# Twelve groups of TensorE products whose results nobody reads, taken out of the last block of a four-layer kernel

## The chip, the cores and the metric

The kernel runs on one core of one Trainium2 chip, as one launch. The metric is the device time of that core in microseconds; several executions are measured and their median is given. One further execution is taken with the hardware profiler, and all profile lines come from that one.

## The reference, cut to what matters

The input `x` has 128 sequences of 64 tokens with 256 features. Four conditioned layers follow each other, each added to its own input:

```python
x = x + L0(x, cond_512, ...)      # self-attention, 16 heads, per-sequence modulated weights
x = x + L1(x, cond_512, ...)      # a bottleneck of 64 with per-sequence weights
x = x + L2(x, ids, states, ...)   # layer norms with gathered tables, then an MLP and a layer norm
x = x + L3(x, cond_512, ...)      # a rank-30 per-sequence weight
```

The change lies at the seam between the last two. The end of L2 and all of L3 are

```python
def _mlp_ln(s, W1, b1, W2, b2, g, b):
    h = jax.nn.silu(s @ W1 + b1) @ W2 + b2
    return _ln(h, g, b)                    # (h - mean) * rsqrt(var + eps) * g + b

U = (mu @ W_dec + b_dec).reshape(B, IN_DIM + 1, K)     # K = 30
param = jnp.einsum('bik,kj->bij', U, V)
out = jnp.einsum('bsd,bde->bse', x, param[:, :-1, :]) + param[:, -1, :][:, None, :]
```

## The kernel before, in words

The 8192 tokens are cut into 16 blocks of 512 tokens (8 sequences). A prologue computes all that depends on the condition alone. Then each block goes through `attention(blk)` (L0) and `rest(blk, ...)` (L1, L2, L3). Inside a block, a "tile" is 128 tokens, so there are four tiles, `tl` = 0 to 3; feature-major arrays are held in two halves, `c` = 0 and 1.

**Order of the work.** Nothing is issued while the Python functions run. Each call of `pe`, `dve`, `act`, `pool` or `load` records an operation in a `Plan`, with its estimated time, what it reads and writes, and the buffers it needs. `Plan.order()` then simulates the engines and picks, for each engine among the operations that could start now, the one with the lowest number `prio`: the block's number times 400, plus an entry of a table `TURNS` (one table for the prologue, the first, the second, the middle, the last but one and the last block). The resulting list is emitted as it is, so each engine executes its instructions strictly in that list's order. PSUM banks (four buffers called `bank`) go to operations in the order in which they are planned.

**The end of a block.** For the last block, where `quick` is true, the end of L2 and L3 run so:

- L1387 (PE): for each tile, the product of `s2` with `w2` into a bank; L1392 (DVE) adds `b2` and stores `x3[tl]`; L469 and L470 (DVE) compute its mean and variance into `mvy`.
- L474 and L476 (POOL) make `ry`, the reciprocal standard deviation of all four tiles; L1253 and L1254 (POOL) make `nry`, minus the mean times `ry`.
- L1259 (ACT), four times: `yn[tl]`, the normalized tile.
- L1403 and L1406 (POOL), per tile: the product with the gamma `lg`, and the sum with `x2[tl]`, which gives the residual stream token-major in `x3[tl]`.
- L1418 (PE): eight transposes of 128x128, first the four tiles of `c` = 0 and then the four of `c` = 1; L1424 (DVE), once for each `c`, scales by gamma and adds the residual, giving `x3T`.
- L1445 (PE): the products with `uT`, 32 small matmuls; L1456 (DVE) adds the bias into `zT`; L1471 (PE): the products with `vw` into four banks.
- L1479 (DVE), per tile: bank plus `x3[tl]`; L1483 (SP): the output DMA of that tile.

In the profile these buffers carry the name of the slot that they sit in: `uu`, `uv` and `p` are pools of slots that are inherited by `x3`, `h`, `s2` and others once their first use is over. So `uu` or `p` in a line is often `yn` or `x3`.

**The products that nobody reads.** The helper `keep(n, gate)` (L437 to L449) takes a bank, multiplies four columns of a value `gate` with the identity (L444), and then multiplies the identity with itself `n` times (L446). Nothing reads the bank afterwards. The L444 matmul waits until the gate's value is there. `keep` records its operation as one of the prologue, with the table entry -500, so it comes ahead of any operation of the last block that could start at the same moment on PE. In the last block it is called six times: with `n` = 4 for `mvy`, `ry` and `nry`, and with `n` = 3 for `yn[0]`, `yn[1]` and `yn[2]`. In fp32 each of these matmuls appears twice in the profile (2 and 8 for `n` = 4; 2 and 6 for `n` = 3).

Of the kernel before, what the change touches and what calls it, by code (L numbers as in the profile page):

```python
# [22 lines left out]
NTILE = T // 128  # L23
# [35 lines left out]
class Plan:  # L59
# [19 lines left out]
    def op(self, eng, took, emit, reads=(), writes=(), busy=None, claims=(), full=0.0, mode=0, pair=False, dma=0.0, table=0):  # L79


        k = self.noted[self.blk] = self.noted.get(self.blk, -1) + 1
        o = dict(eng=eng, took=took, busy=took if busy is None else busy, emit=emit, full=full, mode=mode, pair=pair, dma=dma, table=table)
        o.update(blk=self.blk, k=k, n=len(self.ops), deps=set(), turn=set(), bufs=[], new=[])
        for wr, us in ((False, reads), (True, writes), (False, [(b, "claim") for b in claims])):
            for u in us:
                buf, part = u if isinstance(u, tuple) else (u, None)
                if buf.fixed and part == "claim":
                    continue
                if not buf.seen:  # L90
                    o["new"].append(buf)
                elif buf.seen[0][0] is not o:
                    o["turn"].add(buf.seen[0][0]["n"])
                for other, p, w in buf.seen:
                    if other is not o and (w or wr) and (p is None or part is None or p == part):
                        o["deps"].add(other["n"])
                if wr or not buf.fixed:
                    buf.seen.append((o, part, wr))
                    if buf not in o["bufs"]:
                        o["bufs"].append(buf)  # L100
                        buf.left += 1
        self.ops.append(o)
# [117 lines left out]
    -30847 -21098 5029 39705 -29888 -33414 17870 15965 21160 18587 23602 29288 20398 29675 -32783 -14063 -2864 31417  # L220
    17450 17488 -15993 28657 -41896 -7536 -19666 21238 -40657 411 24862 11649 -23801 10654 8695 15478 -14178 -28768
    -42626 -13379 -20998 18401 -17670 15952 -3416 12222 20491 37701 1362 -22594 -9529 15406 6194 21828 27928 25779
    -10633 41137 464 10909 -44878 -11608 -42604 -45090 10155 -44468 -500 -500 -500 -500 -500 -500
    """,
    "first": """
    16883 -4343 14529 16216 12997 362 17988 20162 -39793 -680 16016 -20705 24354 5226 -12605 14786 19988 -2731 30982
# [85 lines left out]
def resid_chain(ctx: ExitStack, tc: tile.TileContext, a: dict, out: bass.AP, nblk: int = NBLK):  # L312
# [8 lines left out]
    nc = tc.nc  # L321
# [7 lines left out]
    ident = const.tile([128, 128], F32, name="ident", tag="ident")  # L329
# [100 lines left out]
    plan = Plan(kinds, turns, {"p1": list(HEIRS_1), "p2": list(HEIRS_2), "uu": list(HEIRS_U), "uv": list(HEIRS_V)})  # L430
    op = plan.op

    def pe(us, f, reads, writes, claims=(), full=1.0, mode=0):

        op("PE", us + 0.16, f, reads, writes, busy=us, claims=claims, full=full, mode=mode)

    def keep(n, gate):  # L437


        ps, blk = Buf("bank"), plan.blk  # L440
        plan.blk = -1

        def products():
            nc.tensor.matmul(ps.t[:, :4], ident, gate[1](), start=True, stop=True)  # L444
            for k in range(n):
                nc.tensor.matmul(ps.t[:, bass.ts(k, 128)], ident, ident, start=True, stop=True)  # L446

        pe(0.12 * n, products, [gate[0]], [ps])
        plan.blk = blk  # L449

    def dve(n, f, reads, writes, more=0.0, pair=False):

# [7 lines left out]
    def pool(us, f, reads, writes):  # L460
        op("POOL", us + 0.1, f, reads, writes, busy=us)
# [729 lines left out]
    def rest(blk, x1T, pw, oh, wdn, wup, tab, uT):  # L1191

        b0 = blk * NB
        quick = blk == nblk - 1
# [56 lines left out]
        def offset(mv, r, nr):  # L1251

            pool(0.24, lambda: nc.gpsimd.tensor_scalar(nr.t, mv.t[:, :, 0], -1.0, None, ALU.mult), [mv], [nr])  # L1253
            pool(0.24, lambda: nc.gpsimd.tensor_tensor(nr.t, nr.t, r.t, ALU.mult), [nr, r], [nr])  # L1254

        def normalize(dst, src, r, nr, tl):
            act(
                256,
                lambda: nc.scalar.activation(  # L1259
                    dst.t, src.t, AF.Identity, bias=nr.t[:, tl : tl + 1], scale=r.t[:, tl : tl + 1]  # L1260
                ),
                [src, r, nr],
                [dst],
                more=0.186,
            )

        x2, xn, h = ([Buf(k) for _ in range(NTILE)] for k in ("x2", "xn", "h"))
        for tl in range(NTILE):
            ps = Buf("bank")
# [32 lines left out]
        for dst, src in ((xnT, xn), (hnT, h)):  # L1302
            for c in range(C):
                ps = Buf("bank")
# [7 lines left out]
        for j, src, dst in ((1, xnT, gs), (2, xnT, xnT), (0, hnT, hnT)):  # L1312
            for c in range(C):
                ps = Buf("bank")
# [20 lines left out]
        for fc in range(C):  # L1335
            ps, th = Buf("bank"), Buf("tmp")
# [42 lines left out]
        mvy, ry, nry = Buf("mvy"), Buf("ry"), Buf("nry")  # L1379
        x3 = [Buf("x3") for _ in range(NTILE)]  # L1380
        yn = [Buf("h") for _ in range(NTILE)] if quick else x3
        for tl in range(NTILE):
            ps = Buf("bank")
# [9 lines left out]
            stats(x3[tl], mvy, tl)  # L1393
        rstd(mvy, ry)
        offset(mvy, ry, nry)
        if quick:
            for value in (mvy, ry, nry):
                keep(4, (value, lambda value=value: value.t.rearrange("p n k -> p (n k)")[:, :4] if value is mvy else value.t))
        for tl in range(NTILE):
            normalize(yn[tl], x3[tl], ry, nry, tl)  # L1400
            if quick and tl < NTILE - 1:
                keep(3, (yn[tl], lambda tl=tl: yn[tl].t[:, :4]))
            pool(0.65, lambda tl=tl: nc.gpsimd.tensor_tensor(x3[tl].t, yn[tl].t, lg, ALU.mult), [yn[tl]], [x3[tl]])  # L1403
            pool(
                0.65,
                lambda tl=tl: nc.gpsimd.tensor_tensor(x3[tl].t, x3[tl].t, x2[tl].t, ALU.add),  # L1406
                [x3[tl], x2[tl]],
                [x3[tl]],
            )
# [3 lines left out]
        for c in range(C):  # L1413
            ps = Buf("bank")
# [23 lines left out]
        ps, zT = Buf("bank"), Buf("zT")  # L1438
# [26 lines left out]
        for two in range(2):  # L1465
# [8 lines left out]
            for i in range(2):  # L1474
                tl = 2 * two + i
                n = blk * NTILE + tl
# [11 lines left out]
    for blk in range(nblk):  # L1488
        plan.blk = blk
        rest(blk, *attention(blk))  # L1490
# [118 lines left out]
```

## Time and profile before

| what | value |
|---|---|
| median of 3 runs | 900.8 us (897.63 to 904.46) |
| profiled execution, its own time | 894.98 us |
| span of that execution in the profile | 893.2 us |
| mean granted TensorE clock | 0.984 |
| PE busy | 830.2 us (93%) |
| DVE, POOL, ACT busy | 638.4, 608.0 and 446.9 us |
| last products of L1387 end | about 875.1 us after the span's start |
| first transposes of L1418 start | 884.52 us |
| last output DMA issued | 890.27 us |

The span runs from the first to the last instruction of the core; the profiled execution's own time is 1.78 us longer. Times in the views count from the span's start. "Granted clock" is the share of full speed that TensorE's throttle granted in a stretch. PE means matmuls, PEld the loads of their weights. A line number is that of the kernel before; in the changed kernel the lines after the helper are 14 lower, and those after the removed calls 19 lower. In the kernel before, the program's last PE instructions stand in this order: L1387, then six times L444 with its L446, then L1418, L1445 and L1471.

### The profile page before, as it was taken

How to read it: one execution, taken by the hardware profiler on the slowest of the kernel's cores; microseconds unless marked ns; L12 is line 12 of the kernel's file. 1: busy time of each engine (PE TensorE's matmuls, PEld its weight loads, DVE VectorE, ACT ScalarE, POOL GpSimd, SP SyncE). 2: the span in 40 equal slices, each digit the busy share in tenths (PEclk: the TensorE clock that was granted, in tenths of full speed). 3: DMA queues.
4: the chain of work that ended last, by engine and by line, in shares of the span. 5: the costliest groups of instructions: out<-in, count | busy, mean ns of one | idle time of the engine just before them, and what ended most of it. 6: DMA issues, size and time to landing. Idle time of an engine off the chain costs nothing.

```text
span 893.2 us, 24076 instructions
## 1 busy us (share of the span) xinstructions
PE 830.2 (93%) x9806; PEld 539.8 (60%) x9806; DVE 638.4 (71%) x1365; ACT 446.9 (50%) x825; POOL 608.0 (68%) x826
## 2 busy tenths in 40 slices
PE   4669999999999999999999999999999999999886
PEld 3548746656665756666566657566666667565435
DVE  3779867868685878777785858777776858586533
ACT  1454444545564555545555645555555556453330
POOL 5563673949687695959596886959595968845333
PEclk9889999999999999999999999999999999999998
DMA  8768742233423242332334232423324332102000
GB/s 252 210 160 251 243 127 64 67 85 103 123 84 116 73 119 82 95 94 73 117 88 125 85 111 69 128 77 92 101 74 117 84 97 84 48 11 64 1 24 25
DMA packets 62575, 90.24 MB, mean 101 GB/s; under 512 B 6328, under 2 KB 46200, under 8 KB 62464
## 3 DMA queue, kind: packets, MB, share of 16 engines
q1 hardware_dynamic: 57344, 71.92, 28.1%
q0 software_dynamic: 5120, 16.78, 6.0%
q8 instruction: 77, 1.26, 0.6%
q14 instruction: 34, 0.28, 0.1%
HBM read 75.44 MB, written 13.24 MB: 99 GB/s over the span
## 4 chain that ended last, share of the span: by engine, by line
PE 54%; POOL 18%; DVE 13%; ACT 6%; issue 5%; DMA 3%; SPq 0%; DVEq 0%; ACTq 0%; POOLq 0%
PE bank L1344 19%; PE sc L1071 4%; PE bank L982 4%; PE bank L1387 4%; PE bank L1015 4%; PE bank L1146 4%; DVE mt L1080 3%; POOL wdn L956 2%; PE sc L1121 2%; POOL kxe L1029 2%; PE bank L1058 2%; PE bank L1176 2%; POOL uu L1290 2%; PE bank L1317 1%; POOL xsT L925 1%
## 5 line engine op out<-in xcount | busy, mean ns | idle before, releaser
L1135 ACT ACTIVATE e<-sc 128x1024 f32<-128x1024 f32 x128 | 125.9, 1023 | 78.3 <-PE sc L1121 78.3
L1080 DVE TENSOR_REDUCE mt<-sc 128x8 f32<-128x1024 f32 x128 | 151.9, 1205 | 16.2 <-PE sc L1071 13.6
L1165 POOL TENSOR_TENSOR att<-ao,rz 128x256 f32<-128x256 f32 x45 | 28.1, 625 | 76.2 <-DVE rz L1162 75.9
L1326 DVE TENSOR_TENSOR uu<-uu,bank 128x512 f32<-128x512 f32 x96 | 63.9, 681 | 16.4 <-PE bank L1317 15.8
L1015 PE MATMUL bank<-wk,xsT 128*128 128x256 f32 x256 | 71.0, 413 | 0.9 <-POOL xsT L925 0.8
L1344 PE MATMUL bank<-uu,w_s 128*128 128x512 f32 x128 | 66.7, 604 | 0.8 <-DVE uu L1326 0.8
L1344 PE MATMUL bank<-uu,w_t 128*128 128x512 f32 x128 | 65.0, 618 | 0.5 <-DVE uu L1326 0.5
L1344 PE MATMUL bank<-x2T,w_x 128*128 128x512 f32 x128 | 64.7, 607 | 0.0
L1387 PE MATMUL bank<-w,uu 128*128 128x256 f32 x256 | 61.8, 385 | 1.9 <-DVE uu L1362 1.9
L1015 PEld LDWEIGHTS bank<-wk,xsT 128*128 128x128 f32 x256 | 48.8, 202 | 19.1 <-issue 11.1
L982 PE MATMUL bank<-osT,wo 128*128 128x512 f32 x128 | 59.2, 604 | 0.5 <-DVE osT L1181 0.5
L1344 PE MATMUL bank<-uu,w_h 128*128 128x512 f32 x128 | 58.7, 595 | 0.5 <-DVE uu L1326 0.4
L474 POOL TENSOR_SCALAR ry<-mvy 128x4 f32<-128x4 f32 (+1 forms) x19 | 4.4, 232 | 77.7 <-DVE mvy L470 77.6
L1090 ACT COPY mt<-mt 128x16 f32<-128x16 f32 x64 | 13.1, 204 | 84.4 <-DVE mt L1080 84.4
L469 DVE BATCH_NORM_STATS2 st<-uu 128x6 f32<-128x256 f32 x119 | 48.5, 418 | 8.1 <-ACT uu L1276 5.0
L1029 POOL TENSOR_TENSOR kxe<-kxe,kbr 128x256 f32<-128x256 f32 x64 | 46.8, 732 | 9.0 <-DVE kxe L1023 6.6
L1387 PEld LDWEIGHTS bank<-w,uu 128*128 128x128 f32 x256 | 45.9, 190 | 9.4 <-DVE uu L1362 3.1
L1023 DVE TENSOR_TENSOR kxe<-bank,dmk 128x256 f32<-128x256 f32 x64 | 26.8, 419 | 30.3 <-PE bank L1015 25.6
L956 POOL TENSOR_TENSOR wdn<-gdb,late 128x512 f32<-128x512 f32 x32 | 40.6, 1272 | 11.4 <-PE bank L1205 6.0
L940 POOL DMA_INDIRECT pw<-in_pw,idx x39 | 40.0, 1024 | 8.0 <-issue 7.4
L970 POOL TENSOR_TENSOR wup<-wup,ubb 128x512 f32<-128x512 f32 x32 | 40.6, 1269 | 3.7 <-DMA ubb<-ugub 1.5
L1103 ACT ACTIVATE mX<-bank,early 128x128 bf16<-128x128 f32 x64 | 23.6, 369 | 38.3 <-PE bank L1096 38.3
(217 smaller groups left out, 2135.9 us busy)
## 6 DMA issues: line engine op xcount, KB each, us to landing
xT<-in_xT SPq DMA_DIRECT2D x32, 256.0 KB
gdb<-dgdb SPq DMA_DIRECT2D x16, 512.0 KB
ubb<-ugub SPq DMA_DIRECT2D x32, 256.0 KB
wup<-ugub SPq DMA_DIRECT2D x32, 256.0 KB
dmk<-demod_k SPq DMA_DIRECT2D x30, 256.0 KB
out_x<-uu SPq DMA_DIRECT2D x35, 128.0 KB
ud<-uu SPq DMA_DIRECT2D x8, 512.0 KB
uT<-ud SPq DMA_DIRECT2D x16, 256.0 KB
```

Of the source, the lines that this page charges most:

```text
L469: dve(256, lambda: nc.vector.bn_stats(st.t, x.t), [x], [st])
L940: lambda tl=tl, n=n: nc.gpsimd.indirect_dma_start(out=pw[tl].t, out_offset=None, in_=a["pw"], in_offset=bass.IndirectOffsetOnAxis(ap=idx[: ...
L956: lambda w=w, dp=dp: nc.gpsimd.tensor_tensor(w(), gdb.t[:, :, 0:64], dp, ALU.mult),
L970: pool(1.25, lambda w=w: nc.gpsimd.tensor_tensor(w(wup), w(wup), w(ubb), ALU.add), [wup, ubb], [wup])
L982: nc.tensor.matmul(ps.t, owT[:, c, bass.ts(oc, 128)], osT.t[:, c, :], start=(c == 0), stop=(c == C - 1))
L1015: nc.tensor.matmul(ps.t[:, :F], xsT.t[:, c, bass.ts(tl, 128)], kwT[:, c, :], start=(c == 0), stop=(c == C - 1))
L1029: lambda: nc.gpsimd.tensor_tensor(kxe.t[:, :, 0:D], kxe.t[:, :, 0:D], heads(kinds["kbr"][0]), ALU.add),
L1080: lambda two=two: nc.vector.tensor_reduce(mt.t[:, two, 0:4], sc.t[:, two, :].rearrange("p q (g n) -> p q g n", g=4), AX.X, ALU.max),
L1135: lambda k=k: nc.scalar.activation(es[k].t, sc.t[:, 2 * k : 2 * k + 2, :], AF.Exp, scale=0.25),
L1326: lambda ps=ps, src=src, dst=dst, c=c: nc.vector.tensor_tensor(dst.t[:, c, :], src.t[:, c, :], ps.t, ALU.mult),
L1344: lambda ps=ps, w=w, src=src, fc=fc, c=c, n=n: nc.tensor.matmul(ps.t, w.t[:, c, bass.ts(fc, 128)], src.t[:, c, :], start=(n == 0 and c == ...
L1387: nc.tensor.matmul(ps.t[:, :F], s2.t[:, c, bass.ts(tl, 128)], w2.t[:, c, :], start=(c == 0), stop=(c == C - 1))
```

## The change

The helper `keep`, its six calls and its six table entries are taken out. The change is described as "the last block without the unread products; the orders of the last two blocks searched anew", but nothing else in the source differs: the tables of the last two blocks hold the same numbers in both kernels. When both kernels are built and their instructions are laid side by side, engine by engine, DVE, ACT, POOL and SP have the same instructions in the same order over the whole program; PE has the same order without the twelve rows of L444 and L446.

```diff
-    -10633 41137 464 10909 -44878 -11608 -42604 -45090 10155 -44468 -500 -500 -500 -500 -500 -500
+    -10633 41137 464 10909 -44878 -11608 -42604 -45090 10155 -44468
...
-    def keep(n, gate):
-
-
-        ps, blk = Buf("bank"), plan.blk
-        plan.blk = -1
-
-        def products():
-            nc.tensor.matmul(ps.t[:, :4], ident, gate[1](), start=True, stop=True)
-            for k in range(n):
-                nc.tensor.matmul(ps.t[:, bass.ts(k, 128)], ident, ident, start=True, stop=True)
-
-        pe(0.12 * n, products, [gate[0]], [ps])
-        plan.blk = blk
-
...
         rstd(mvy, ry)
         offset(mvy, ry, nry)
-        if quick:
-            for value in (mvy, ry, nry):
-                keep(4, (value, lambda value=value: value.t.rearrange("p n k -> p (n k)")[:, :4] if value is mvy else value.t))
         for tl in range(NTILE):
             normalize(yn[tl], x3[tl], ry, nry, tl)
-            if quick and tl < NTILE - 1:
-                keep(3, (yn[tl], lambda tl=tl: yn[tl].t[:, :4]))
```

In the built program the first four transposes now carry waits of their own: each waits for ACT's normalize of its tile. Before, only the fourth did, since the products ahead of it had waited for the other three.

## The prediction

> **What bounds the kernel now.** I read the page first: PE is busy 93% of the span, so TensorE bounds the kernel as a whole. But the change touches only the last 20 us, where PE's work is partly products without a reader, so the share of busy time says nothing here. I therefore took the chain that ended last, in order of time, for the tail; each row is a start, a length and what the chain passed through.
>
> ```profile
> 875.09 0.42 DVE p L1392
> ...
> 876.82 1.01 POOL ry L476
> 877.84 0.04 issue
> 877.88 0.39 PE bank L444 x2
> 878.26 1.54 PE bank L446 x8
> 879.81 0.22 PE bank L444 x2
> 880.03 1.91 PE bank L446 x8
> 881.94 0.18 PE bank L444 x2
> ...
> 884.68 0.45 PE bank L1418 x4
> 885.13 0.03 issue
> 885.16 1.42 DVE uu L1424 x2
> 886.58 0.04 issue
> 886.62 0.59 PE bank L1445 x24
> ```
>
> The reader is to see that from 877.88 to 884.4 the chain runs through nothing but the products of L444 and L446: they are not beside the path, they are the path. The transposes of L1418 stand behind them on an engine that works in order. What the transposes really need is shown by the timeline of ACT and POOL:
>
> ```profile
> 879.63 0.58 ACT L1259 ACTIVATE uu<-p,nry,ry 128x256 f32<-128x256 f32 x1
> ...
> 883.72 0.72 POOL L1406 TENSOR_TENSOR uu<-uu,p 128x256 f32<-128x256 f32 x1
> ```
>
> The four normalizes end at 878.74, 879.23, 879.72 and 880.21 (starts 878.14, 878.65, 879.14, 879.63; lengths 0.60 and 0.58). So the last input of the transposes exists at 880.21, and the first one runs at 884.52. In the view of waits over this stretch the same delay stands on the other side:
>
> ```profile
> DVE uu L1424 <- PE bank L1418: 9.0, 1, 9.0
> ```
>
> The products' own price depends on TensorE's clock, so the last view is PE in stretches of 3.41 us: the stretch, its length, PE's busy time with the number of instructions, the granted clock, and the share and rate of the DMAs:
>
> ```profile
> 868.32:871.73 3.41, 2.00 (x7) 1.00 0.00 0
> 871.73:875.15 3.42, 3.42 (x19) 1.00 0.00 0
> 875.15:878.56 3.41, 1.71 (x15) 1.00 0.00 0
> 878.56:881.97 3.41, 3.41 (x19) 0.50 0.02 5
> 881.97:885.39 3.42, 3.42 (x31) 1.00 0.00 0
> 885.39:888.80 3.41, 1.74 (x42) 1.00 0.00 0
> ```
>
> The clock changes at 878.56, 881.97 and 888.8, that is, in steps of one such stretch: a stretch that was busy for half its length (1.71) is followed by one at half speed, a stretch that was full by one at full speed. The products after the half-speed stretch run at full speed, and so do L1418, L1445 and L1471.
>
> [...]the stretch from 851.25 to 854.67 was busy for 2.13 us, half of it (1.06) transposes of L1308, and the next one ran at 0.50; the one from 868.32 with 2.00 us of plain products was followed by 1.00. [...]
>
> **The change part by part.** The order of the other four engines is the same in both built programs, and that of PE is the same without the twelve rows, so up to 874.8 the two kernels do the same work in the same order. I price everything before at nothing: the tables of the last two blocks are not altered, though the change's description speaks of searched orders.
>
> *Removed:* 12 rows in L444, 42 in L446, from 874.80 to 884.4. The first group (gate `mvy`, 1.4 us) lies in a gap in which PE has nothing else, and is worth nothing. The rest holds the transposes back.
>
> *What is late next:* the chain L1259. The fourth normalize lands at 880.21. The transposes of `c` = 0 for tiles 0 to 2 run before that, one by one as the normalizes come (0.5 us apart, which covers one cold transpose at 0.22 each). So one transpose of `c` = 0 and four of `c` = 1 are left at 880.25.
>
> *Added:* nothing is issued, but the tail loses its warm clock. PE has no work from 875.06 to 878.8, 3.7 us; then five of eight transposes are left. By the stretches above I take clock 0.50 for all that follows. What it costs, from rows at both clocks:
>
> - Transposes. Four L1058 transposes took 1.12 us at 0.50 (at 58.70) and 0.66 warm (at 783.17): 0.22 or 0.11 apart, and 0.46 or 0.33 for the last one's length. Cold, one transpose from its weight load to DVE's start is 0.23 + 0.46 + 0.04 = 0.73, so L1424 for `c` = 0 starts at 880.98 and ends at 881.69. The four of `c` = 1 end 4 x 0.22 = 0.88 later, at 881.83; L1424 for `c` = 1 runs from 881.87 to 882.58.
> - L1445. No cold row of it exists. Warm its last 24 take 0.59: 0.37 of issue and 0.22 of the last one's length. Bounds: 0.59 if only latency counts, 1.18 at plain doubling. I take 0.37 x 2 + 0.28 = 1.02, since the drain is not all clocked work (0.33 to 0.46, not to 0.66, above). Start 882.62, end 883.64.
> - L1456: 0.02 + 0.30 + 0.04, as before, to 884.00.
> - L1471. Again no cold row with all eight; warm 0.78 = 0.30 issue + 0.48. Bounds 0.78 and 1.56. I take 0.60 + 0.59 = 1.19, to 885.19; L1479 starts at 885.22.
>
> Before, L1479 starts at 888.40. The gain is 888.40 - 885.22 = 3.2 us; with both bounds at plain doubling 2.6 us (885.75), with L1445 and L1471 warm 4.0 us (884.38).
>
> *Cover for the rest.* L1479 also reads `x3[tl]`, whose last sum on POOL ends at 884.44, for tile 3; POOL's order does not depend on PE here. Tile 3 is reached about 1.1 us after L1479's first start (889.48 against 888.40), at 886.3, so 1.9 us of slack remain. In the warmest case, 884.38 + 1.1 = 885.5, it is still 1.0. From L1479 on (four adds, four output DMAs of 128 KB, no other transfer in flight) nothing changes: last DMA issued 890.27, span's end 893.2. No wait is added behind which anything queues: the three new waits on the first transposes hold only transposes back.
>
> Sum: span 893.2 - 3.2 = 890.0 us, own time 894.98 - 3.2 = 891.8 us. The median of the three runs before is 5.8 us above the profiled execution, so in medians I carry the difference over: 900.8 - 3.2 = 897.6 us. About 1% (9 us) is what a measurement of this kernel can tell from no change, and the runs before lie 6.8 us apart; the gain is a third of one per cent.
>
> **The rivals.**
>
> *The products were cheap in most executions.* [...]Warm, the groups cost 1.1, 1.1 and three times 0.90 (882.62 to 883.52) from 877.88: the transposes would start at 882.8 and not 884.5, so before would be 1.6 us faster than profiled, and the gain only 3.2 - 1.6 = 1.6 us: 899.2 us. [...]against: the profiled execution is cold.
>
> *The tail stays warm.* If the transposes[...] bring the clock to 1.00 by 882, the gain is 4.0 us, 896.8 us. Against: at most 1.76 us of cold transposes fall into that window, and the trace went cold after 1.71 and 2.13.
>
> *Slower: the clock falls lower than half.* PE's work from 880.25 on is, warm, about 0.66 for five transposes, 0.59 and 0.78, together 2.03 us; DVE's steps and the gaps are 1.15. Before has 888.40 - 880.25 = 8.15 us for it. The change loses from a slowing of (8.15 - 1.15) / 2.03 = 3.4 on, a granted clock under 0.29. [...]No stretch of this trace shows a clock under 0.50.
>
> *The change reaches further than the tail*, by the searched orders it speaks of. The side-by-side order excludes it[...].
>
> **How the numbers follow.** Cold tail against cold products 0.58 (897.6); products mostly warm before 0.27 (899.2); warm tail 0.08 (896.8); [...]something unseen 0.04. [...]the likeliest's own bounds are 896.8 to 898.2. A median of few runs that lie 6.8 us apart is uncertain by some 2 to 3 us, which I add below: 894.2 to 901.4. Faster by over 1% needs 9 us, three times the gain: 0.04, from the unseen and from the spread. Slower by over 1%: 0.02. Within 1%: 0.94.
>
> **What would show it right or wrong.** Right: no L444 or L446; the four L1259 end near 880.2; three transposes run singly between 878.8 and 880.2; the clock is 0.50 from about 878.6 on to the end; L1424 starts near 881.0, L1479 near 885.2, POOL's last sum still at 884.4, the span ends near 890.0. The step on the clock is wrong if L1471 takes 0.78 at 1.00; the step on POOL is wrong if L1479's last add is released by POOL; the whole is wrong if L1424 does not start before 884, or if spans differ before 874.8 by as much as the gain.

## The result and the profile after

| | before | after | ratio |
|---|---|---|---|
| first set, 14 runs each | 903.02 us | 901.59 us (897.82 to 904.63) | 0.9978 [0.9957, 0.9998] |
| second set (49 runs of before, 22 of after) | 893.09 us | 890.84 us (888.46 to 894.55) | 0.9976 [0.9964, 0.9987] |
| profiled execution, first set | 894.98 us, span 893.2 us | 902.43 us, span 900.6 us | |

The brackets hold 95% intervals. One of the 49 runs, 1070.64 us long at a granted clock of 0.753, is left out of the ratio. What was taken out are six groups with 54 rows in the profile, 12 of L444 and 42 of L446: the "twelve" of the title counts the rows of L444.

The change gains 0.2%, about 2 us. Its profiled execution was nevertheless 7.4 us longer than that of before. So spans must not be compared here; the tail must be. I count from the end of the last product of L1387 (L1373 after), which ends at 875.06 us in the profile of before and at 885.15 us in that of after: 10.1 us were lost ahead of any changed instruction. Times of the tail, and ends of spans counted from there, are taken from the unrounded records; the rows shown here can differ by 0.01 us.

The two rows of before between which the change lies:

```profile
871.34 3.73 PE bank L1387 x16
...
888.40 0.47 DVE p L1479 x2
```

The chain that ended last, after, in order of time (start, length, what it passed through):

```profile
881.43 3.73 PE bank L1373 x16
...
888.24 0.61 ACT uu L1245
...
890.37 1.34 PE bank L1399 x5
...
891.73 0.76 DVE uu L1405
...
892.54 0.91 PE bank L1426 x24
...
893.82 1.30 PE bank L1452 x8
...
895.16 0.47 DVE p L1460 x2
```

The products are gone from it: PE comes right behind the normalizes of ACT. L1460 starts at 895.16, 10.01 us after the last product of L1373; before it was 888.40 - 875.06 = 13.34. The forecast was 13.34 - 3.18 = 10.16. The view of waits has the same on its other side, 4.6 us instead of 9.0:

```profile
DVE uu L1405 <- PE bank L1399: 4.6, 1, 4.6
```

The clock, in stretches of 3.41 us, the length of the one at 0.50 in the profile of before (stretch, length, PE busy and instructions, granted clock, DMA share and rate):

```profile
884.36:887.77 3.41, 0.79 (x4) 1.00 0.00 0
887.77:891.18 3.41, 2.24 (x7) 0.50 0.00 0
891.18:894.59 3.41, 2.59 (x43) 0.50 0.02 5
894.59:898.00 3.41, 0.47 (x8) 0.50 0.36 120
```

Half speed holds from 887.77 to the end, as forecast. L1426 took 0.91 us (estimated 1.02) and L1452 took 1.30 (estimated 1.19).

**The end of the span.** Between L1460's start and the span's end lie 5.49 us after, but 4.81 before. The queue instructions of the program's last line show why (count, durations in ns as least, median and most, first and last start in us). Before:

```profile
L1605 POOLq DRAIN  x3: 45/102/6078, 883.7 to 892.9; - x3
L1605 SPq DRAIN  x3: 7/7/7, 892.4 to 892.7; - x3
```

After:

```profile
L1586 POOLq DRAIN  x3: 45/102/6075, 893.8 to 900.4; - x3
L1586 SPq DRAIN  x3: 7/7/7, 899.2 to 900.1; - x3
```

POOL drains for 6.08 us from the issue of its last sum on. Before, that ended at 883.7 + 6.1 = 889.8, well ahead of SP, which had seen the last output landed at 892.4. After, it ends at 893.8 + 6.1 = 899.9, and SP had been ready at 899.2. The drain is the new end of the program, and it takes back 0.7 us. Counted from the last product of L1387 the span ends after 18.15 us before and 15.50 us after: the net gain is 2.7 us, not 3.2.

### The profile page after: what moved, and what is told of

Read it like the earlier page. It is cut to its first block, busy times and chain, and to the rows that moved or that the text cites. A ratio compares the mean times of both kernels' runs of the same rounds, so it can differ in the third digit from the quotient of the medians.

```text
span 900.6 us, 23967 instructions
## 1 busy us (share of the span) xinstructions
PE 832.6 (92%) x9752; PEld 535.5 (59%) x9752; DVE 636.7 (71%) x1365; ACT 447.6 (50%) x825; POOL 608.1 (68%) x826
## 4 chain that ended last, share of the span: by engine, by line
PE 76%; DVE 10%; ACT 7%; issue 3%; POOL 2%; DMA 2%; SPq 0%; DVEq 0%; ACTq 0%; POOLq 0%
PE bank L1330 21%; PE sc L1057 8%; PE bank L1001 7%; PE bank L968 6%; PE bank L1373 6%; PE bank L1132 6%; DVE mt L1066 4%; PE bank L1044 2%; PE sc L1107 2%; PE bank L1162 2%; ACT uu L1297 2%; PE bank L1209 2%; PE bank L1399 2%; PE bank L1303 2%; PE bank L1191 2%
## 5 line engine op out<-in xcount | busy, mean ns | idle before, releaser
L1373 PE MATMUL bank<-w,uu 128*128 128x256 f32 x256 | 61.8, 385 | 1.9 <-DVE uu L1348 1.9
L1373 PEld LDWEIGHTS bank<-w,uu 128*128 128x128 f32 x256 | 45.9, 190 | 9.4 <-DVE uu L1348 3.1
```

The costliest lines, as they stand in the source:

```text
L1373: nc.tensor.matmul(ps.t[:, :F], s2.t[:, c, bass.ts(tl, 128)], w2.t[:, c, :], start=(c == 0), stop=(c == C - 1))
```

## The experiments

Times "after E" are counted from the end of the last product of L1387, E; the table at the end of this section gathers them. Whole times are comparable only within a set, since the sets did not all run on one chip. The kernels with only the groups of `yn`, with only the other three groups, with two POOL operations more, and the two repetitions of before ran once each: only their tails are read.

**The changed kernel again** (no edit).

> The changed kernel once more. Tail theory (the products stood on the path, the tail without them runs at half clock): L1460 starts 10.0 us after the last product of L1373 ends (885.16 to 895.16 in the first profile), granted clock 0.50 from the transposes on; against 13.34 us in the profile of before. In the whole time 3 us less than before, ratio about 0.9965. Rival (the products were cheap in most executions): tail the same 10.0, but a ratio nearer to 0.998. Where the two programs' orders are the same, the spans may differ by up to 10 us either way; theory of the gathers: the DVE reduce L1066 that stands behind the matmuls L1057 starts 0.3 to 2.4 us after POOL's second gather L926 of its block, a different delay in each block, and the sum of these delays over the blocks explains the span.

Measured: L1460 at 10.01 us after E, the span's end at 15.51, ratio 0.9976 [0.9964, 0.9987]. The tail repeats to 0.01 us. Here the profiled span was 888.2 us: E came at 872.73, 12.4 us earlier than in the first profile of the same program. The tail of the changed kernel is settled; what moves E is not the change, and the run without gathers below is about that.

**Products that hold nothing up.**

The helper `fill`, not shown, is built like `keep`: one product that waits for `x3[2]`, then FILL = 15 products of the identity with itself, which run behind the last L1387.

```diff
+            if quick and tl == 2:
+                fill(FILL, x3[tl])
...
                     nc.tensor.transpose(ps.t[:, bass.ts(tl, 128)], yn[tl].t[:, bass.ts(c, 128)], ident)
+                    if quick and c == 0 and tl < NTILE - 1:
+                        nc.tensor.matmul(ps.t[:, bass.ts(tl + 1, 128)], ident, ident, start=True, stop=True)
...
+                    for _ in range(2 * (quick and r == 0 and c == 0)):
+                        nc.tensor.matmul(ps.t[:, 256:384], ident, ident, start=True, stop=True)
```

> The changed kernel with products without a reader that hold nothing up: 15 right behind the last L1387, waiting only for tile 2 of x3, to fill the gap until the first normalize; one between each two of the first four transposes; two ahead of L1446. Tail theory: with the clock at 1.00 throughout, L1479 (here L1480 or so) starts 8.8 us after L1387's end instead of 10.0[...]. Rival (the half clock costs nothing here): 10.0. In the whole time 1 us less than the changed kernel, which five rounds hardly resolve.

Measured: L1480 at 8.81 us after E, with the clock at 1.00 up to there. The end of its chain:

```profile
877.71 0.58 PE bank L1446 x24
...
878.67 0.78 PE bank L1472 x8
...
879.49 0.47 DVE p L1480 x2
```

The rows are those of a warm tail (0.58 and 0.78 against 0.91 and 1.30 above). So the half clock costs 1.2 us in the changed kernel (10.01 against 8.81). But the whole time did not follow: 891.73 us, ratio 0.9980 [0.9969, 0.9990] against 0.9976 of the changed kernel in the same set, and the span ends 15.50 us after E, as in the changed kernel. The drain shows where the 1.2 us went:

```profile
L1606 POOLq DRAIN  x3: 45/102/6078, 879.3 to 885.9; - x3
L1606 SPq DRAIN  x3: 7/7/7, 883.6 to 885.6; - x3
```

SP was ready at 883.6, and POOL's drain held the end until 879.3 + 6.1 = 885.4.

**Twice the products.**

```diff
-                nc.tensor.matmul(ps.t[:, bass.ts(k, 128)], ident, ident, start=True, stop=True)
+                nc.tensor.matmul(ps.t[:, bass.ts(k % 4, 128)], ident, ident, start=True, stop=True)
...
-                keep(4, (value, ...))
+                keep(8, (value, ...))
...
-                keep(3, (yn[tl], ...))
+                keep(6, (yn[tl], ...))
```

> The kernel before with twice as many products in each group (8 for mvy, ry and nry, 6 for each yn). Tail theory: the doubled mvy group (18 rows at 0.11, 2.0 us) still fits into the gap; the other groups grow by 34 rows of 0.11 to 0.22 us, so L1479 starts 16.5 to 18.5 us after L1387's end instead of 13.3, and the whole time is 3 to 5 us above before, ratio 1.003 to 1.006. Rival (PE's products are hidden behind POOL's chain of L1403 and L1406): 13.3 and ratio 1.000.

Measured: L1479 at 15.51 us after E, the span's end at 20.32, ratio 1.0036 [1.0016, 1.0055]. The rival is refuted: the products stand on the path, and doubling them costs 2.2 us of tail, and 1.4 to 4.9 us of time by the interval. It costs less than forecast because the clock was 1.00 throughout, with PE idle for 0.80 us ahead of the group for `ry` where it was idle for 1.70 in before: 34 rows that I had priced at 0.11 to 0.22 us ran at 0.11, and the old ones became cheaper too.

**Only the groups of `yn`.**

```diff
-            for value in (mvy, ry, nry):
+            for value in ():
```

> The kernel before without the products for mvy, ry and nry; the three groups for yn stay. Tail theory: they start at 3.7 us after L1387's last product on a clock that is or turns 0.50, 8 rows of 0.22 us each, so the transposes follow at 8.1 to 9.1 us and L1479 starts at 12.0 to 13.6 us; the three groups alone cost two thirds or more of what all six do. Rival (the first three groups hold the transposes back, the later ones fit behind them): about 10.0.

Measured: L1479 at 12.88 us after E. The chain:

```profile
880.18 0.59 PE bank L444 x2
880.77 1.49 PE bank L446 x6
...
883.96 0.22 PE bank L444 x2
884.18 1.42 PE bank L446 x6
885.60 0.45 PE bank L1418 x4
```

Each group takes 1.6 to 2.1 us at half clock, and the transposes wait for all three. These three groups alone cost 12.88 - 10.01 = 2.87 of the 3.33 us.

**Only the groups of `mvy`, `ry` and `nry`.**

```diff
-            if quick and tl < NTILE - 1:
+            if False:
                 keep(3, (yn[tl], lambda tl=tl: yn[tl].t[:, :4]))
```

> The kernel before without the three groups gated by yn; those for mvy, ry and nry stay. Tail theory: if cold, the groups end 6.4 us after L1387's last product and L1479 starts at 10.3 to 10.6 us; if warm, they end at 5.0, before the last normalize, hold nothing back and keep the clock, and L1479 starts at 9.0 to 9.3 us, earlier than in the changed kernel (10.0). Rival (all six groups cost alike): half of the difference, 11.7 us.

Measured: L1479 at 10.66 us after E, just above the cold case: the groups ran at 0.50 from 3.4 to 6.8 us after E, ended at 6.95, and the tail behind them ran at 1.00. They cost 0.65 us against the changed kernel. The two halves do not add up, 2.87 + 0.65 against 3.33. Behind each half alone, as behind both, the clock was 1.00, against 0.50 in the changed kernel. Why the halves do not add up, no run separates.

**The kernel before, twice more** (no edit).

> The kernel before once more, for the clock in its tail. [...]L1479 starts either about 13.3 us after L1387's last product, with a stretch of 3.4 us at 0.50 during the products, or, with the clock at 1.00 throughout, at about 11.7 us; the span then ends 18.1 or 16.5 us after it, so that the change is worth 2.7 or 1.0 us, with the drain as the limit of the kernel after. Rival (always cold): 13.3.

> As before_2: 13.3 us with a cold stretch, or 11.7 us without one; an execution between them only where the cold stretch begins or ends within the products.

Measured: 13.34 us in both, with a stretch at 0.50 beginning 3.7 and 4.0 us after E (3.5 in the first profile), the span's end at 18.15 in both. All three profiles of before ran their products cold in part. The 11.7 us of the warm case was my estimate from the rows at 1.00; no run shows it. In the other kernels whose tails went cold the clock fell from 2.1 us after E (`yn` groups only) to 3.9 (no gathers), and in the changed kernel at 2.6 in one profile and 3.8 in the other; the three falls of before lie within 3.5 to 4.0. Whether before runs warm in executions in which the fall would come at another time stays open.

**Two POOL operations more at the end.** Nothing reads what they write.

```diff
...
+            pool(0.65, lambda: nc.gpsimd.tensor_tensor(yn[3].t, x3[3].t, lg, ALU.mult), [x3[3]], [yn[3]])
+            pool(0.65, lambda: nc.gpsimd.tensor_tensor(yn[3].t, yn[3].t, lg, ALU.mult), [yn[3]], [yn[3]])
...
```

> The changed kernel with two more POOL operations of 0.72 us at its end, which nothing reads. Theory of the drain: POOL's last operation ends 10.8 us after the last product of L1373 instead of 9.4 and the span ends 16.9 us after it instead of 15.45, although L1460 still starts at 10.0. Rival: 15.45.

Measured: L1465, the add, starts at 10.01 us after E as in the changed kernel, and the span ends at 16.74 us, 1.24 later, as POOL's last operation does (10.63 against 9.39). The end follows POOL:

```profile
L1591 POOLq DRAIN  x3: 45/102/6635, 896.6 to 903.7; - x3
L1591 SPq DRAIN  x3: 7/7/7, 901.3 to 903.5; - x3
```

Its drain begins 1.3 us before the last operation ends (896.6 and 897.91), where it begins 0.8 us before that in the changed kernel (893.79 and 894.54), and it lasts 6.64 us instead of 6.08. But it ends 5.3 us after the last operation's end in both (after: 899.86 - 894.54; this one: 903.23 - 897.91).

**Two tiles' residual sums on DVE, with and without the filling products.**

```diff
+            if quick and tl < 2:
+                dve(256, lambda tl=tl: nc.vector.tensor_tensor(x3[tl].t, yn[tl].t, lg, ALU.mult), [yn[tl]], [x3[tl]])
+                dve(256, lambda tl=tl: nc.vector.tensor_tensor(x3[tl].t, x3[tl].t, x2[tl].t, ALU.add), [x3[tl], x2[tl]], [x3[tl]])
+                continue
             pool(0.65, lambda tl=tl: nc.gpsimd.tensor_tensor(x3[tl].t, yn[tl].t, lg, ALU.mult), [yn[tl]], [x3[tl]])
...
```

> The changed kernel, with the residual sums L1384 and L1387 of tiles 0 and 1 of the last block moved from POOL to DVE, which has nothing to do there; POOL keeps tiles 2 and 3. Theory of the drain (at the end of the program POOL drains for 6.1 us, 5.3 us of them after its last sum, and the span cannot end before; in the changed kernel this and not the output DMAs ends the span): POOL's last sum ends 7.6 us after the last product of L1373 instead of 9.4, the output DMAs end the span again, and it ends 14.8 us after that product instead of 15.45. The step to L1460 stays at 10.0. Rival (the last landing is only slower by chance): 15.45 again, or 14.8 in other kernels of this kind too. In the whole time 0.6 us below the changed kernel.

> Both: the filling products of the run called warm, and the sums of tiles 0 and 1 on DVE. Theory of the drain and tail theory together: L1484 starts 8.8 us after L1387's last product, the drain ends 12.9 us after it, and the span ends 13.6 us after it, 1.8 us earlier than in the changed kernel and 4.5 us earlier than in the profile of before; whole time against before 0.9955. Rival (the end of the span does not follow L1484): 15.5.

Measured: without filling, the add at 9.94 us after E and the span's end at 14.75; with it, 8.89 and 13.89. Ratios to before, in one set: 0.9966 [0.9951, 0.9980] and 0.9946 [0.9928, 0.9963]. The second, at 893.78 us against 897.78, has the lowest time in its set, and it does the whole computation; the two intervals overlap. In it drain and outputs are nearly level:

```profile
L1610 POOLq DRAIN  x3: 45/102/6657, 885.6 to 892.8; - x3
L1610 SPq DRAIN  x3: 7/7/7, 892.1 to 892.6; - x3
```

POOL's drain ends at 885.63 + 6.66 = 892.3 and SP is ready at 892.1. So the drain is the end again, and a further gain on PE alone would be worth nothing.

**POOL's gathers replaced.**

```diff
-                lambda tl=tl, n=n: nc.gpsimd.indirect_dma_start(...),
+                lambda tl=tl, n=n: nc.sync.dma_start(out=pw[tl].t, in_=a["pw"][0:128, :]),
```

> The changed kernel with POOL's four gathers per block replaced by four contiguous loads of the first 128 rows of the same table, issued by SP; the rows that the tokens ask for are left out. Theory of the gathers (POOL's gathers delay the DVE reduce L1066 by a varying time, and that makes most of the spread between executions): the reduce starts within 0.3 us of its matmuls in every block, blocks take 49.2 us or less, and the executions spread over 3 us instead of 8 to 11. Rival (the delay comes from elsewhere[...]): delays of 0.5 to 2.4 us remain in some blocks and the spread stays. The tail is that of the changed kernel, 10.0 us.

Measured: 887.92 us, from 886.76 to 889.31 over 6 runs, ratio 0.9939 [0.9920, 0.9958]. The span ends at 14.75 us after E, with POOL's last operation at 9.4 as in the changed kernel: with the long drain gone (POOL's longest is 0.83 us here, and SP is ready at 884.3), the outputs end it. The runs spread over 2.6 us; the changed kernel in the same set spread over 6.1 us, but in 22 runs. From block 3 to block 14, counted from 0, the blocks follow each other 49.2 us apart, where the first profile of after has 49.4 to 51.4 us. The edit also frees POOL of some 66 us of work and puts 64 more transfers on SP. These views explain the 10.1 us by which the profiles of before and after differ ahead of the tail. DVE's timeline of the first profile of after, at one place of two blocks (start, length, what; in brackets the idle time before it):

```profile
430.77 2.35 DVE L1066 TENSOR_REDUCE mt<-sc 128x8 f32<-128x1024 f32 x2 [1.44 <-PE sc L1057]
...
532.56 2.36 DVE L1066 TENSOR_REDUCE mt<-sc 128x8 f32<-128x1024 f32 x2 [2.23 <-PE bank L1044]
```

In the profile of before, at the place of the first:

```profile
425.52 2.36 DVE L1080 TENSOR_REDUCE mt<-sc 128x8 f32<-128x1024 f32 x2 [0.39 <-ACT p L1259]
```

POOL's gather ahead of the second of them:

```profile
530.11 1.07 POOL L926 DMA_INDIRECT pw<-in_pw,idx  x1 [0.17 <-issue]
```

And DVE's timeline without gathers, at the place of the first:

```profile
422.61 2.35 DVE L1061 TENSOR_REDUCE mt<-sc 128x8 f32<-128x1024 f32 x2 [0.17 <-PE sc L1052]
```

In the two profiles with gathers of the first set, the reduce's matmuls end at the same point of these blocks, 0.1 to 0.3 us after POOL's second gather of the block has begun; but the reduce starts late, and by a different time in each block. I summed, over the 128 reduces of a profile, the time between a reduce's start and the later of its last matmul's end and DVE's previous end: 8.1 us in the profile of before, 18.8 in the first profile of after, 8.2 in the second, 6.6 without gathers. The difference of the first two, 10.6 us, is the loss of 10.1 us to within what else moves. The other profiles agree: over all thirteen, E lies between 870.3 and 887.3 us and the sum between 6.6 and 19.7, but E less the sum lies between 862.3 and 867.6. Without gathers no reduce of these blocks is delayed by over 0.3 us. So with the gathers the delay goes. How much of the spread goes with it is not shown, since six runs span less than 22 in any case. By what path the gathers act, and why some executions showed 0.1 to 0.5 us in each block and others 0.5 to 2.2, is not shown either.

| kernel | add starts, us after E | span ends, us after E | last POOL operation ends |
|---|---|---|---|
| before (3 profiles) | 13.34 | 18.15 | 9.4 |
| after (2 profiles) | 10.01 | 15.50, 15.51 | 9.4 |
| filling products | 8.81 | 15.50 | 9.4 |
| twice the products | 15.51 | 20.32 | 9.4 |
| `yn` groups only | 12.88 | 17.70 | 9.4 |
| `mvy`, `ry`, `nry` groups only | 10.66 | 15.67 | 9.4 |
| two POOL operations more | 10.01 | 16.74 | 10.6 |
| two tiles on DVE | 9.94 | 14.75 | 7.8 |
| both | 8.89 | 13.89 | 7.8 |
| no gathers | 10.00 | 14.75 | 9.4 |

## Why the prediction was right or wrong

**Right: what the products cost and what takes their place.** They stood on the path (twice as many: 2.2 us more), the tail without them runs at half clock, and L1460 starts 10.01 us after E where 10.16 was worked out. Term by term: the first L1405 at 5.73 (5.92 forecast), L1437 at 8.33 (8.60), L1452 at 8.67 (8.94). The two rows without a cold example came out at -0.11 and +0.12 us against the forecast; that these cancel in the sum is luck. The price of the cold clock, which the rival "the tail stays warm" puts at 0.8 us for L1445 and L1471 alone, is 1.2 us by the filling products, which also warm the transposes.

**Wrong: "From L1479 on (...) nothing changes".** The step on cover asked of POOL only when its last sum is done (884.44, with 1.9 us of slack), not when POOL itself is done. Its drain, 6.08 us long, stood in the trace of before at 883.7, in the queue's instructions and not among the busy groups, and ended 2.6 us before SP was ready. A gain of 3.3 us had to run into it. It cuts the gain from 3.3 to 2.7 us, and it makes the gain of the rival "the tail stays warm" worth nothing: the kernel with filling products reached 8.81 and ended as late as the changed one. That the drain is the end is shown from three sides: with POOL's work ending later the span ended later (16.74), with POOL's work ending earlier it ended earlier (14.75), and without the gathers and their long drain too (14.75).

**Wrong: the base of the sum.** The predicted 897.6 us hung on the median of three runs, 900.8 us. Over 14 runs before has 903.02, 2.2 us more, and the range's upper end, 901.4, lay 0.2 us below the measured 901.59. Of the 4.0 us between the forecast and the measured median, 2.2 are this and 1.8 the smaller gain (903.02 - 901.59 = 1.4 by the two medians). The drain explains 0.5 of these 1.8; the rest lies within the spread of the runs and stays open. The step that failed is "A median of few runs that lie 6.8 us apart is uncertain by some 2 to 3 us": it was counted once, but two medians enter, the one carried over and the one forecast. The gain, 3.2 us, lies within the first set's interval (0.2 to 3.9 us) and at the edge of the second's (1.2 to 3.2 us); the tail's 2.7 us lies inside both.

**Not shown: what makes the clock fall.** The prediction set a stretch busy for 2.13 us, half of it transposes, with 0.50 behind it, beside one with 2.00 us of plain products and 1.00 behind it. That the transposes make the difference is not shown. The same trace has a stretch that speaks against it: the one from 451.91 to 455.32 was busy for 2.44 us, all but 0.40 of it transposes (L1096, L1176, L1273, L1418), and the next ran at 1.00. Nor does the busy time of one stretch tell: 2.47 us were followed by 0.50 in before (151.52 to 154.93), 1.77 us by 1.00 in after (850.22 to 853.64). So the cold tail, my estimate from the stretches with 1.71 and 2.13 us, came true, but from no safe mark; what makes the clock fall stays open.

**Priced at nothing: all that comes before the change.** The prediction named as a sign of being wrong that spans differ before 874.8 by as much as the gain. They did, by 10.1 us. But two profiles of the same changed program differ there by 12.4 us, so this is not the change.

**Open.** The rival with cheap products in most executions forecast 1.6 us, also inside both intervals; with the drain as the end it would be worth only some 1.0 (16.5 - 15.5), just below the second interval. The three cold profiles of before do not settle it, since all three falls lie at 3.5 to 4.0 us after E. The best witness is the kernel with both edits: it gains 3.3 to 6.5 us by its interval, where the tails give 18.15 - 13.89 = 4.3 for a cold before and 1.6 less, 2.7, for a warm one. That speaks against a before that is warm in most executions; some may be. The rival on a clock lower than half did not happen: no tail showed less than 0.50.

## What to carry to other kernels

Products without a reader that are to keep TensorE's clock up (1.00 with the filling products, 0.50 in the tail without) should end before the work that they warm could start. Here 54 rows gated by the same values as the real work held it back by 4.5 us (13.34 against 8.81, with the rows behind them warm in both) to save 1.2, a net loss of 3.3. The same idea placed in the gap gains the 1.2 us up to the first add; of these, 0.9 reached the span's end once POOL's work ended earlier (14.75 against 13.89). Before pricing the end of a kernel, read the queue instructions of the last line for every engine: what an engine still has to drain is no busy time (6.08 us on POOL here), and it can be the next end. Where executions of one program differ by more than the effect sought, anchor at an instruction just ahead of the change and compare intervals from there.

## What the runs showed of the hardware that was not expected

- POOL's drain at the end of the program ends 5.3 us after its last operation in eight of the nine kernels here with gathers; that of the ninth, with only the `mvy`, `ry` and `nry` groups, is not shown. Without gathers the longest drain is 0.83 us, and it ends 0.1 us after the last operation:

```profile
L1581 POOLq DRAIN  x3: 39/78/829, 879.0 to 884.8; - x3
```

- A reduce on DVE whose matmuls end while POOL issues a gather starts late, with no other wait that the profile shows: in the middle blocks by 0.1 to 0.5 us in the profile of before and by 0.5 to 2.2 us in the first of after. Without gathers it starts there within 0.3 us.
- The clock fell to 0.50 at 2.1 to 4.0 us after E in every tail in which PE stood idle for 1.7 us or more ahead of the normalizes, and did not fall there in the three kernels (filling products with and without the two tiles on DVE, 0.2 us, and twice the products, 0.8 us) that left it less. In the changed kernel it stayed at 0.50 through stretches that were busy for 2.24 and 2.59 of 3.41 us; in before it came back after one that was busy throughout (3.41 us from 878.56 on).
